# Two context attentions of a perceiver block: a later settle and a lag of two, weighted values by halves, denominators copied out of PSUM, pools that wait by tile

## The chip, the cores and the metric

The kernel runs on one core of a Trainium2 chip. A core has a matrix engine (TensorE, in the profile PE for the multiplications and PEld for the loads of the stationary operand), a vector engine (VectorE, DVE), a scalar engine (ScalarE, ACT), a general engine (GpSimd, POOL) and a queue for transfers (SyncE, SP). Each engine works through its own instructions in order; an instruction waits on semaphores for what it needs. Matrix products land in PSUM, a small memory of eight banks; everything else on the core lies in SBUF.

The metric is the device time of one execution in microseconds. Before the change three runs took 1695.6, 1703.4 and 1700.06 us, with a median of 1700.06.

## The reference

Two layers work on 512 tokens of width 512 (`x`), with a context of 8192 tokens of the same width. Everything is float32. Each layer adds three things to `x`, each after a layer norm: an attention over the context, an attention among the tokens, and a mixture of eight experts of which each token uses two. Cut to the part that is changed:

```python
x = x + L0_xattn(layernorm(x), ctx, padding_mask)   # 16 heads of 32, queries and keys normed per head
x = x + L0_attn(layernorm(x))                       # each token sees itself and later ones
x = x + L0_ffn(layernorm(x))                        # top 2 of 8 experts, width 2048
x = x + L1_xattn(layernorm(x), ctx, mask)           # 16 heads of 32, no norm of the keys
x = x + L1_attn(layernorm(x))                       # a band of 64 neighbours
x = x + L1_ffn(layernorm(x))                        # top 2 of 8 experts, width 1024

def xattn(q, y):                                    # both context attentions
    s = einsum("bihd,bjhd->bhij", heads(q), heads(k(y))) * scale
    p = softmax(where(allowed, s, -inf))
    return einsum("bhij,bjhd->bihd", p, heads(v(y))) @ Wo.T + bo
```

The masks come as data. With the inputs of this case only a small part of the context can be seen by any token.

## The kernel before

**Slots.** The kernel finds out at run time which tiles of 128 context tokens hold anything that may be seen. It has room for 15 such tiles, the *slots* (`SLOTS`), and gathers them; `tile_list` (L568) builds the list of tiles from counts. The list for layer 1 needs all of that layer's mask, which `MaskScan` (L1185) reads piece by piece during layer 0's key loop (the squares on ACT that find out whether a column is the same for all queries); its `finish` (L1216) and `tile_list` make the list. If 15 slots are not enough, another path runs under a branch at the end (L2028); it is not taken here.

**The order of stages**, in the profiled execution: queries and constants up to about 78 us; layer 0's key loop to about 213; its attention to about 484; self-attention to about 640; experts to about 935; layer 1's context attention to about 1365, of which the key loop runs to about 1100; self-attention to about 1478, and experts to the end.

**attend_slots** (L742) is called by both context attentions (`cross_slots0`, `cross_slots1`) with functions of the caller. Heads come in `NG` = 4 groups of `GH` = 4; the four heads of a group are four small products that run beside each other in the array, and such a set is called a *quad* here. An f32 product of 512 columns is two records (two passes) in the profile, so a quad is eight records.

- *Key loop.* For every slot s: `keys(s)` projects the keys (in layer 0: a product in the bank "acc", and DVE adds the bias into `kb`, L1055), `settle` transposes the normed keys of an earlier slot (`ktp`, L1064) and ACT writes them to `kT`, `maxima(0, ...)` multiplies an earlier slot's keys with the queries of group 0 and DVE takes the running maximum of the scores (`take`, L768 and L770), `values` projects the values (`pv`, L1016), and `unit(s)` norms the keys (a square on ACT, then DVE; its last step is L1109). In layer 1 there is no norm, `keys` writes `kT` itself, and `settle` and `unit` do nothing. `beside()` is the mask scan in layer 0.
- *After the loop* the last settles, maxima and values follow, and the first parts of `shift_of(0)` (L646): eight transposes of the maxima for each of its two parts (`mtp`), reductions on DVE (`neg`), a split of the maximum into three bf16 parts on POOL, and a last transposition (`stp`) that yields `shift`, three rows to be subtracted from the scores by a small product.
- *60 attention steps* (L891), one for each group g and slot i. The first 41 are *combined*: two halves j, in each of which PE makes a quad of two score heads of group g (`sc`) and two score heads of a later group (`scm`, for its maxima), then two small products that subtract the shift (L644); ACT takes the exponentials of the two heads into `pT` (L874), DVE the two maxima. The `sc` tiles have four PSUM banks, the `scm` tiles three, `acc` one. In the last 19, *plain* steps, PE makes the four score heads of g alone.
- `accumulate` (L821) multiplies the exponentials of the step before with the values: a quad over all 512 queries into `acc`. After a group's last slot ACT copies `acc` to `o` (L836).
- `add_up` (L838) adds the exponentials of four slots into one tile (POOL, in the last group DVE), so that `denominators` (L850) has to sum only four tiles per group by products with ones (`den`, in one of the four banks of `sc`).
- *Fillers* run at the end of a step, one at most: the parts of the next group's shift, the denominators (three steps after the end of a group), two reciprocals by halves (`divide`, L861), the output projections (`ops`, L717), and in layer 0's steps from 2 on a piece of layer 1's list (`listing`, L1084). In the last group a part of the denominators is made at the end of the last two steps.

**Pools.** Tiles come from pools that open and close with the stages. When a pool is opened where a closed one lay, its tiles wait for the users of what lay there before.

Of the kernel before, what the change touches and what calls it, by code (L numbers as in the profile page):

```python
# [57 lines left out]
def tile_perceiver(  # L58
# [6 lines left out]

    const = ctx.enter_context(tc.tile_pool(name="const", bufs=1))
# [9 lines left out]
    dram = ctx.enter_context(tc.tile_pool(name="dram", bufs=1, space=bass.MemoryType.DRAM))  # L76
# [22 lines left out]
    with tc.tile_pool(name="begins", bufs=1) as tmp, tc.tile_pool(name="beginsps", bufs=1, space=PSUM) as tps:  # L99
# [322 lines left out]
    def cross_attention0():  # L422
        with ExitStack() as st:
            pool = st.enter_context(tc.tile_pool(name="c0", bufs=2))
            ctxp = st.enter_context(tc.tile_pool(name="ctxp0", bufs=2))
            psum = st.enter_context(tc.tile_pool(name="c0ps", bufs=2, space=PSUM))
            pacc = st.enter_context(tc.tile_pool(name="c0acc", bufs=1, space=PSUM))
# [3 lines left out]
            with tc.tile_pool(name="c0q", bufs=2) as qp:  # L431
# [8 lines left out]
            kvp = st.enter_context(tc.tile_pool(name="c0kv", bufs=NCHUNK // 2))  # L440
# [70 lines left out]
    def cross_attention1():  # L511
        with ExitStack() as st:
            pool = st.enter_context(tc.tile_pool(name="c1", bufs=2))
            ctxp = st.enter_context(tc.tile_pool(name="ctxp1", bufs=2))
            psum = st.enter_context(tc.tile_pool(name="c1ps", bufs=2, space=PSUM))
            pacc = st.enter_context(tc.tile_pool(name="c1acc", bufs=1, space=PSUM))
# [3 lines left out]
            with tc.tile_pool(name="c1q", bufs=2) as qp:  # L520
# [7 lines left out]
            kvp = st.enter_context(tc.tile_pool(name="c1kv", bufs=NCHUNK))  # L528
            mp = st.enter_context(tc.tile_pool(name="c1m", bufs=2))
# [38 lines left out]
    def tile_list(tmp, psum, counts, bad, tag, out):  # L568
# [8 lines left out]
        nc.tensor.transpose(tp, counts, ident)  # L577
        nc.vector.tensor_copy(rows, tp)
# [4 lines left out]
        nc.tensor.matmul(ps, lhsT=tri, rhs=some, start=True, stop=True)  # L583
        place = tmp.tile([n, 1], F32, name="place", tag="place")
# [7 lines left out]
        nc.tensor.matmul(ps[:, SLOTS : SLOTS + 1], lhsT=ones[0:n, 0:1], rhs=some, start=True, stop=True)  # L592
        row = tmp.tile([1, SLOTS + 1], F32, name="row", tag="row")
# [10 lines left out]
        ps = psum.tile([P, SLOTS], F32, name="kbp", tag=tag)  # L604
        nc.tensor.matmul(ps, lhsT=rows, rhs=taken, start=True, stop=True)
        kbias = small.tile([P, SLOTS], F32, name="kbias", tag="kbias")
        nc.vector.tensor_scalar(kbias, ps, 1.0, BIG, ALU.subtract, ALU.mult)
# [134 lines left out]
    def attend_slots(pool, psum, pacc, kT, vN, qT, kbias, wo, bv, late, keys, settle, values, unit, more, early, aside, beside, extra):  # L742
# [47 lines left out]
        for s in range(n):  # L790
            keep(keys, s)
            if s >= 1:
                settle(s - 1)
            if s >= 2:
                maxima(0, s - 2)
            if (s + 1) * loop // n > s * loop // n:
                keep(values, todo.pop(0))
            unit(s)
            if s == 3:
                aside()  # L800
            beside()
        settle(n - 1)
        steps = shift_of(0)
# [3 lines left out]
        keep(values, todo.pop(0))  # L807
# [11 lines left out]
        last = None  # L819

        def accumulate():  # L821

            if last is None:
                return
            g, i, pT = last
            if i == 0:
                k.sums[g] = pacc.tile([P, S], F32, name="acc", tag="acc")
            for h in range(GH):
                nc.tensor.matmul(  # L829
                    k.sums[g][HD * h : HD * (h + 1), :],  # L830
                    lhsT=vN[:, i, g * P + HD * h : g * P + HD * (h + 1)],
                    rhs=pT[:, h, :], start=(i == 0), stop=(i == n - 1),
                )
            if i == n - 1 and g < NG - 1:
# [15 lines left out]
        def denominators(g, which, end):  # L850

            for j in which:
                if j == 0:
                    dens[g] = psum.tile([P, S], F32, name="den", tag="s")
                for h in range(GH):
# [3 lines left out]
                    )  # L859

        def divide(g, i):  # L861

            r = slice(i * S // 2, (i + 1) * S // 2)
            if i == 0:
                dens[g, 0] = late().tile([P, S], F32, name="d", tag="d", bufs=1)
# [1290 lines left out]
```

## Time and profile before

| | |
|---|---|
| median of three runs | 1700.06 us |
| the profiled execution's own time | 1700.19 us |
| its span | 1698.5 us |
| mean granted clock of TensorE | 0.938 |
| layer 0 key loop, 78 to 213 us: PE busy, PEclk, DMA share | 122.24 of 135.00, 0.94, 0.43 |
| layer 0 attention, 213 to 406: PE busy, PEclk | 190.14 of 193.00, 0.97 |
| its end, 406 to 484: PE busy, PEclk | 71.03 of 78.00, 0.96 |
| between experts and layer 1's keys, 935 to 965: PE busy, PEclk | 20.10 of 30.00, 0.83 |
| layer 1 attention, 1100 to 1284: PE busy, PEclk | 183.17 of 184.00, 0.98 |
| its end, 1284 to 1365: PE busy, PEclk | 73.79 of 81.00, 0.94 |

Busy time of an engine is the time in which at least one of its instructions ran; PE counts as busy while products run, and PEclk is the share of its full clock that was granted. In a stage where PE is busy for nearly the whole time, the pace may still be set by a wait within a quad, since one late head of four leaves the other three running. A line of the waits view names the waiting instruction, what it waited for, the sum, the number of times and the longest. In the timeline view a line is a run of like instructions: start, length, engine, line, operation, output and inputs, shapes and their number, and in brackets the idle time before and what ended it. In the windows view each engine's busy time in a stretch stands in the order PE, PEld, DVE, ACT, POOL, each with its number of instructions in brackets, then PEclk, the DMA engines' mean share and GB/s.

### The profile page before, as it was taken

How to read it: one execution, taken by the hardware profiler on the slowest of the kernel's cores; microseconds unless marked ns; L12 is line 12 of the kernel's file. 1: busy time of each engine (PE TensorE's matmuls, PEld its weight loads, DVE VectorE, ACT ScalarE, POOL GpSimd, SP SyncE). 2: the span in 40 equal slices, each digit the busy share in tenths (PEclk: the TensorE clock that was granted, in tenths of full speed). 3: DMA queues.
4: the chain of work that ended last, by engine and by line, in shares of the span. 5: the costliest groups of instructions: out<-in, count | busy, mean ns of one | idle time of the engine just before them, and what ended most of it. 6: DMA issues, size and time to landing. Idle time of an engine off the chain costs nothing. (4 is left out here: it accounts for less than half of the span.)

```text
span 1698.5 us, 24206 instructions
## 1 busy us (share of the span) xinstructions
PE 1559.3 (92%) x9877; PEld 908.3 (53%) x9877; DVE 775.3 (46%) x1394; ACT 570.7 (34%) x1081; POOL 446.5 (26%) x345
## 2 busy tenths in 40 slices
PE   5888999999979996999999799999999989779996
PEld 2333333333234446999998456433333245369995
DVE  5466677774633655111112133667765526831112
ACT  1356355556622231111111211155556612211110
POOL 6000057787110011000002100078786010010002
PEclk9999989999989977999999899899999989879996
DMA  7145200000030004877784400000000040066572
GB/s 249 50 136 180 74 1 1 1 1 1 1 131 1 1 1 177 326 257 267 284 293 155 156 26 19 25 1 1 1 1 1 1 152 11 25 237 216 187 246 92
DMA packets 83928, 169.32 MB, mean 100 GB/s; under 512 B 5106, under 2 KB 20498, under 8 KB 82384
## 3 DMA queue, kind: packets, MB, share of 16 engines
q1 hardware_dynamic: 77200, 147.87, 25.4%
q0 software_dynamic: 6016, 17.55, 3.0%
q10 hardware_dynamic: 576, 2.10, 0.4%
q8 instruction: 84, 1.38, 0.3%
q14 instruction: 52, 0.43, 0.1%
HBM read 156.82 MB, written 9.63 MB: 98 GB/s over the span
## 5 line engine op out<-in xcount | busy, mean ns | idle before, releaser
L874 ACT ACTIVATE pT<-sc,kbias 128x512 f32<-128x512 f32 x480 | 299.4, 687 | 205.3 <-PE sc L644 142.8
L757 PE MATMUL sc<-qTf,kTf 32*128 32x512 f32 x1264 | 299.4, 660 | 6.1 <-DVE d L866 4.9
L770 DVE SCALAR_TENSOR_TENSOR mx<-scm,kbias,mx 128x512 f32<-128x512 f32 x312 | 215.4, 743 | 98.2 <-PE scm L757 95.8
L757 PE MATMUL scm<-qTf,kTf 32*128 32x512 f32 x656 | 241.2, 654 | 2.1 <-DVE mx L770 2.1
L1801 PE MATMUL y<-hT,w 128*128 128x112 f32 (+13 forms) x1536 | 211.0, 297 | 0.6 <-DVE hT L1976 0.6
L1785 PE MATMUL hps<-tokens,w 128*128 128x112 f32 (+13 forms) x1536 | 208.5, 295 | 0.0
L1801 PEld LDWEIGHTS y<-hT,w 128*128 128x128 f32 x1536 | 204.3, 197 | 2.5 <-DVE hT L1976 0.8
L1785 PEld LDWEIGHTS hps<-tokens,w 128*128 128x128 f32 x1536 | 201.5, 195 | 1.7
L847 POOL TENSOR_TENSOR four<-four,pT 128x2048 f32<-128x2048 f32 x42 | 190.7, 4540 | 9.7 <-ACT pT L874 6.7
L757 PEld LDWEIGHTS sc<-qTf,kTf 32*128 32x128 f32 x1264 | 91.3, 190 | 147.8 <-issue 111.5
L847 POOL TENSOR_TENSOR four<-pT 128x2048 f32<-128x2048 f32 x24 | 109.0, 4544 | 109.2 <-ACT pT L874 109.2
L829 PE MATMUL acc<-pT,vNf 128*32 128x512 f32 x960 | 133.7, 623 | 1.5 <-ACT o L836 1.5
L770 DVE SCALAR_TENSOR_TENSOR mx<-sc,kbias,mx 128x512 f32<-128x512 f32 x136 | 93.3, 744 | 80.3 <-PE sc L757 80.3
L1976 DVE TENSOR_TENSOR hT<-sg,hps 128x264 f32<-128x264 f32 (+7 forms) x64 | 28.0, 437 | 189.5 <-ACT sg L1975 189.5
L644 PE MATMUL sc<-shift,ones 3*128 3x512 bf16 (+3 forms) x544 | 100.1, 383 | 3.6 <-DVE shift L679 3.6
L757 PEld LDWEIGHTS scm<-qTf,kTf 32*128 32x128 f32 x656 | 75.0, 188 | 49.8 <-DVE mx L770 38.0
L1826 POOL DMA_DIRECT2D answers_d<-yb x17 | 9.5, 559 | 311.5 <-ACT yb L1819 311.4
L1975 ACT ACTIVATE sg<-hps 128x264 f32<-128x264 f32 (+7 forms) x64 | 25.4, 397 | 137.4 <-PE hps L1785 137.4
L829 PEld LDWEIGHTS acc<-pT,vNf 128*32 128x32 f32 x960 | 20.7, 109 | 88.0 <-issue 80.6
L658 DVE TENSOR_REDUCE neg<-mtp 128x4 f32<-128x512 f32 x64 | 41.2, 683 | 53.8 <-PE mtp L655 53.8
L1981 DVE TENSOR_TENSOR hT<-sg 128x224 f32<-128x224 f32 (+7 forms) x32 | 14.7, 459 | 107.6 <-ACT sg L1980 107.6
L1016 PE MATMUL pv<-wkvf,cslot 128*128 128x512 f32 x120 | 59.1, 639 | 0.2 <-ACT vNf L1025 0.2
(340 smaller groups left out, 1833.8 us busy)
## 6 DMA issues: line engine op xcount, KB each, us to landing
w<-in_L_ffn_W SPq DMA_DIRECT2D x96, 1024.0 KB, 7.4
mi<-in_mask SPq DMA_DIRECT2D x32, 512.0 KB, 4.2
cslot<-in_ctxT SPq DMA_DIRECT2D x30, 256.0 KB, 4.9
answers_d<-yb POOLq DMA_DIRECT2D x15, 256.0 KB, 7.1
answers_d<-zero POOLq DMA_DIRECT2D x9, 256.0 KB, 6.6
wkvf<-in_L_xattn_WkvT ACTq DMA_DIRECT2D x4, 512.0 KB, 6.5
wq<-in_L_xattn_WqT SPq DMA_DIRECT2D x2, 1024.0 KB, 7.5
wof<-in_L_xattn_WoT SPq DMA_DIRECT2D x2, 1024.0 KB, 4.7
```

Source lines behind the costliest of these rows:

```text
L644: nc.tensor.matmul(ps, lhsT=ones16[r, :], rhs=k.shifts[g][r, 0:w], start=start, stop=stop)
L658: nc.vector.tensor_reduce(neg[:, h, :], tp.rearrange("p (t k) -> p t k", k=P), AX.X, ALU.max, negate=True)
L757: nc.tensor.matmul(ps, lhsT=kT[HD * h : HD * (h + 1), g, i * P : (i + 1) * P], rhs=qT[HD * h : HD * (h + 1), g, :], start=True, stop=stop,)
L770: nc.vector.scalar_tensor_tensor(to, ps, b, to, ALU.add, ALU.max)
L829: nc.tensor.matmul(k.sums[g][HD * h : HD * (h + 1), :], lhsT=vN[:, i, g * P + HD * h : g * P + HD * (h + 1)], rhs=pT[:, h, :], start=(i == ...
L847: engine.tensor_tensor(to, parts[g][-1], pT, ALU.add)
L874: nc.scalar.activation(pT[:, h, :], ps, AF.Exp, bias=kbias[:, i : i + 1])
L1016: last = nc.tensor.matmul(ps.rearrange("p (g n) -> p g n", g=NG), lhsT=src[:, c, s % 2, :], rhs=wkv[:, :, c, i * P : (i + 1) * P], start=( ...
L1785: nc.tensor.matmul(ps[:, j, 0:k], lhsT=w1[:, c, f * P : (f + 1) * P], rhs=tokens[:, c, starts[r] : starts[r] + k], start=(c == 0), stop=(c ...
L1801: nc.tensor.matmul(accs[0][:, d, 0:k], lhsT=w2[:, f, d * P : (d + 1) * P], rhs=hT[:, f, 0:k], start=(c == 0 and f == 0 and d % 2 == 0), st ...
L1975: nc.scalar.activation(sg, ps, AF.Sigmoid)
L1976: nc.vector.tensor_tensor(dst, sg, ps, ALU.mult)
```

## The change

The change touches both context attentions and the kind of wait between pools.

1. Nearly all pools are opened with `reuse_waits="tile"`: a new tile then waits only for those users of earlier tiles that touched its own bytes (in PSUM, its own bank), and no longer for all users of the pool that was there.
2. In the key loop the settle comes two slots after the keys instead of one, and the maxima three slots after instead of two. `kb` has three buffers instead of two. What follows the loop is reordered; the first part of `shift_of(0)` stands directly behind the last maxima.
3. In combined steps `accumulate` covers half of the queries behind each of the two quads, where one product over all queries stood behind the first. In plain steps it works on the exponentials of two steps before, and `pT` has five buffers instead of four. The last group's last denominators come ahead of the last `accumulate`.
4. For the first three groups ACT copies the finished denominators from PSUM to an SBUF tile `d`, and the reciprocals work in place on it.
5. The list of layer 1's tiles is cut into more fillers: a product of PE and the DVE instruction that reads it are in different steps, and one product (`kbp`) is made earlier. The fillers go from six to nine.

```diff
+    def tile_pool(**kw):
+        return tc.tile_pool(reuse_waits="tile", **kw)
...
         nc.tensor.transpose(tp, counts, ident)
+        yield
         nc.vector.tensor_copy(rows, tp)
...
         nc.tensor.matmul(ps, lhsT=tri, rhs=some, start=True, stop=True)
+        yield
         place = tmp.tile([n, 1], F32, name="place", tag="place")
...
         nc.tensor.matmul(ps[:, SLOTS : SLOTS + 1], lhsT=ones[0:n, 0:1], rhs=some, start=True, stop=True)
+        keep = psum.tile([P, SLOTS], F32, name="kbp", tag=tag)
+        nc.tensor.matmul(keep, lhsT=rows, rhs=taken, start=True, stop=True)
+        yield
         row = tmp.tile([1, SLOTS + 1], F32, name="row", tag="row")
...
-        ps = psum.tile([P, SLOTS], F32, name="kbp", tag=tag)
-        nc.tensor.matmul(ps, lhsT=rows, rhs=taken, start=True, stop=True)
...
         for s in range(n):
             keep(keys, s)
-            if s >= 1:
-                settle(s - 1)
             if s >= 2:
-                maxima(0, s - 2)
+                settle(s - 2)
+            if s >= 3:
+                maxima(0, s - 3)
...
+        settle(n - 2)
+        steps = shift_of(0)
+        maxima(0, n - 3)
+        keep(values, todo.pop(0))
         settle(n - 1)
-        steps = shift_of(0)
         maxima(0, n - 2)
         keep(values, todo.pop(0))
         maxima(0, n - 1)
-        keep(values, todo.pop(0))
         steps[0]()
         keep(values, todo.pop(0))
         steps[1]()
...
-        def accumulate():
-            if last is None:
+        def accumulate(lag, halves=(0, 1)):
+            if len(behind) < lag:
                 return
-            g, i, pT = last
-            if i == 0:
+            g, i, pT = behind[0]
+            r = slice(halves[0] * S // 2, (halves[-1] + 1) * S // 2)
+            if i == 0 and halves[0] == 0:
                 k.sums[g] = pacc.tile([P, S], F32, name="acc", tag="acc")
             for h in range(GH):
                 nc.tensor.matmul(
-                    k.sums[g][HD * h : HD * (h + 1), :],
+                    k.sums[g][HD * h : HD * (h + 1), r],
                     lhsT=vN[:, i, g * P + HD * h : g * P + HD * (h + 1)],
-                    rhs=pT[:, h, :], start=(i == 0), stop=(i == n - 1),
+                    rhs=pT[:, h, r], start=(i == 0 and halves[0] == 0), stop=(i == n - 1 and halves[-1] == 1),
                 )
+            if halves[-1] == 0:
+                return
+            behind.pop(0)
...
+            if g < NG - 1:
+                d = late().tile([P, S], F32, name="d", tag="d", bufs=1)
+                nc.scalar.copy(d, dens[g])
+                dens[g] = d
...
-            if i == 0:
-                dens[g, 0] = late().tile([P, S], F32, name="d", tag="d", bufs=1)
-            nc.vector.reciprocal(dens[g, 0][:, r], dens[g][:, r])
+            nc.vector.reciprocal(dens[g][:, r], dens[g][:, r])
...
-            pT = late().tile([P, GH, S], F32, name="pT", tag="pT", bufs=4)
+            pT = late().tile([P, GH, S], F32, name="pT", tag="pT", bufs=5)
...
-                    if j == 0:
-                        accumulate()
+                    accumulate(1, (j,))
...
-                accumulate()
+                accumulate(2)
...
-        accumulate()
+        accumulate(1)
         denominators(NG - 1, range(end - 2, end), end)
+        accumulate(1)
...
-                kb = kvp.tile([P, D], F32, name="kb", tag="kb")
+                kb = kvp.tile([P, D], F32, name="kb", tag="kb", bufs=3)
...
-                more, EARLY, aside, scanned, [listing] * 6,
+                more, EARLY, aside, scanned, [listing] * 9,
```

Inside the scan's `finish` one more `yield` stands between a transposition (`lbp`) and the DVE reduction that reads it. `late()` opens, at its first call after the key loop, the pool in which `pT`, `o`, `d` and the sums of four live, where the key loop's pools lay, and starts the load of the output weights.

## The prediction

> **What bounds the kernel now.** Busy time comes first, then the granted clock along the span (40 slices of 42.5 us).
>
> ```profile
> PE 1559.3 (92%) x9877; PEld 908.3 (53%) x9877; DVE 775.3 (46%) x1394; ACT 570.7 (34%) x1081; POOL 446.5 (26%) x345
> PEclk9999989999989977999999899899999989879996
> ```
>
> TensorE is the bound almost everywhere, so a change pays where PE stands still, or runs at half clock after standing still. The chain of waits covers the end of the program alone. I therefore read PE's waits stage by stage. First the layer 0 key loop (78 to 213 us), then the end of its attention (406 to 484).
>
> ```profile
> PE ktp L1064 <- DVE kb L1109: 12.0, 7, 3.1
> ```
>
> ```profile
> PE ops L717 <- DVE o L691: 4.3, 2, 2.9
> PE sc L757 <- DVE d L866: 1.8, 1, 1.8
> PE acc L829 <- ACT o L836: 0.7, 1, 0.7
> ```
>
> Columns: total us, times, longest. A short wait drags a slower clock behind it; the windows table, whose column PEclk reads 0.50, shows four such windows (length, then busy PE):
>
> ```profile
> 88.10:94.90 6.80, 6.35 (x16) 2.74 (x17) 4.19 (x7) 3.71 (x9) 0.91 (x3) 0.50 0.86 289
> 139.30:142.70 3.40, 3.40 (x11) 1.11 (x4) 2.07 (x4) 3.31 (x8) 0.43 (x2) 0.50 0.78 231
> 436.30:443.10 6.80, 6.80 (x30) 1.59 (x34) 1.95 (x1) 2.42 (x4) 4.64 (x2) 0.50 0.00 0
> 1316.90:1320.30 3.40, 3.40 (x17) 0.81 (x20) 0.69 (x1) 2.25 (x4) 3.30 (x2) 0.50 0.00 0
> ```
>
> Last, the timeline of PE and of DVE in an ordinary combined step:
>
> ```profile
> 334.12 1.06 PE L829 MATMUL acc<-pT,vNf 128*32 128x512 f32 x8
> 335.11 0.70 PE L757 MATMUL sc<-qTf,kTf 32*128 32x512 f32 x2
> 336.09 0.59 PE L757 MATMUL sc<-qTf,kTf 32*128 32x512 f32 x2
> 336.73 1.10 PE L757 MATMUL scm<-qTf,kTf 32*128 32x512 f32 x2
> 338.19 1.06 PE L829 MATMUL acc<-pT,vNf 128*32 128x512 f32 x8
> ```
>
> ```profile
> 336.33 1.41 DVE L770 SCALAR_TENSOR_TENSOR mx<-scm,kbias,mx 128x512 f32<-128x512 f32 x2 [1.34 <-PE scm L757]
> ```
>
> Acc to acc is 4.07 us. Two score quads stand back to back (335.11, 336.09). The fourth "scm" of the pair needs a bank that DVE's take from 336.33 gives up, and starts only at 337.14, or 2.02 after the first quad's start.
>
> **The change, part by part.**
>
> *Settle one slot later.* A settle transposes the keys that DVE has just normalised (L1109); with one more slot between, the result is there a whole slot (some 8 us) earlier than needed, and the 12.0 us go. So do the two half-clock windows of this loop, worth half their length at most: 3.4 + 1.7. Most is 17. What could be late next: per slot PE has about 7.8 us of work, ACT 70.7/15 = 4.7, DVE 86.0/15 = 5.7, with the mask transfers at 43% of the DMA engines; none reaches PE. I take 15, with 12 and 17 as ends. Layer 1's settle is empty: nothing.
>
> *Loop end.* steps[0] now stands right behind the last maxima; its transposes wait for DVE's takes (the first 1.16 us after the scores, 0.74 each), which a value projection of 3.6 us covered. Lost about 1.3 in each attention (1.1 to 1.6): -2.6.
>
> *Halves.* Self-attention's quad over 256 queries is the nearest row: its two passes stand 0.24 and 0.31 us apart, 0.55 in all, against 0.996 for 512. Two halves cost 0.10 more than a whole. A combined step's own work is then 2 x (0.96 scores + 0.31 subtracts + 0.55) = 3.64. Quads follow each other by 1.82, so the wanted bank comes 2.02 - 1.82 = 0.20 after the quad begins; the late score's own 1.05 to its end then sets 1.25, against the 1.27 of the undisturbed path. Hidden: 3.64; not hidden, each quad is late by half of the 0.20, as the next then starts later too: 3.84. DVE's four takes (2.97) and ACT's four exponentials (2.75) fit beneath. I take 3.75. There are 25 plain-looking 4.07 steps in layer 1 and 20 in layer 0, and five with the listing: 50 x 0.32 = 16. Steps with other work had hidden it in the 0.6 of stall and lose cover: four with outputs (5.44 to 5.61), two with denominators (7.08 to 7.24), two with reciprocals, two with the copy of o, in each attention; I put the loss at 3.1 an attention. Net 16 - 6 = **10** (4 to 15).
>
> *Denominators copied by ACT.* Six copies of 0.60 us (the price of ACT's 512-wide copies). They give the "s" bank back before the two reciprocals of 1.75 each, the 1.8 us wait above. In combined steps ACT is half idle, and the copy only delays the reciprocals (in the 3.1 above). In plain steps ACT is the bound (4 x 0.60 = 2.41 a step, PE 2.28), so the copy costs its 0.60.
>
> *Lag of two in plain steps, the last acc behind the last denominators.* Layer 0's steps 47 to 49 take 5.74 + 5.86 + 4.77 = 16.4. Denominators 3.6 + PE's 2.28, two steps at 2.41, and two ACT copies make 11.9: 4.5 less, of which 3.4 is half clock. Layer 1: 14.85 to 11.9. The four steps about the outputs (13.97) become PE's own 4 x 2.28 + 3.95 = 13.1, or 0.7 after a margin; two transposing steps 3.70 to 3.30, 0.8; at the end a reciprocal runs beside the last acc, 1.0. Sum 7.0 and 5.5: **12.5** (8 to 14). The wait of acc for the copy of o stays.
>
> *Listing by more fillers.* Layer 0's steps 3 to 7 take 7.4 us more than five at 4.07. The timeline says why:
>
> ```profile
> 240.91 4.58 DVE L588 TENSOR_SCALAR taken<-steps,place,some 64x15 f32<-64x15 f32 x1
> 249.78 3.55 DVE L601 TENSOR_TENSOR row<-row,none 1x1 f32<-1x1 f32 x1
> ```
>
> ```profile
> 240.94 4.53 POOL L847 TENSOR_TENSOR four<-pT 128x2048 f32<-128x2048 f32 x1 [3.15 <-ACT pT L874]
> 248.81 4.52 POOL L847 TENSOR_TENSOR four<-four,pT 128x2048 f32<-128x2048 f32 x1 [3.33 <-ACT pT L874]
> ```
>
> Two tiny DVE instructions stand until POOL's add ends, with the takes behind them and PE behind these. Here the Trainium skill speaks against the change: "SBUF — State Buffer", section "Who interferes with whom", says that DVE and GpSimd share a port pair under an exclusive lock, taken by two-port copies and scalar operations and by DVE instructions with two SBUF inputs. By it more yields remove neither wait; they only move PE's waits for DVE. By the row alone (7.4 over the even pace) I would book 7. With the new places, "taken" falls in a step without an add, some 2 us before the running one ends, and "row" meets one by chance. I book **5** (2 to 6.5).
>
> The same page lets a DVE instruction with one SBUF input, outside such modes, run free. That matters for the reciprocals, which now read SBUF beside POOL's adds. The trace shows no such reciprocal there; nearest is the reduce of "crow" from SBUF, 278 ns beside an add and 278 without. I take nothing; the upper end is a whole add, 4.5 us, for each of 12, and below nothing there is no reason.
>
> *Pools by tile.* Weights for self-attention may start some 11 us earlier, but after both attentions PE waits for the layer norm's DVE chain, not weights: 0 to 1, taken 0. After the first ffn, Wq of layer 1 is issued at 934.37 and lands at 940.32; DVE branches at 935.52 and goes on at 940.34, in spite of no semaphore on Wq. If DVE's code waits behind that megabyte, an issue some 6 us earlier shortens this; ACT's same branch took 2.47 before the transfer, PE's branch at the end of the program 3.9 without one. Gain 0 to 4.7, taken **2**. Expert weights wait for routing: nothing.
>
> **Sum.** 15 - 2.6 + 10 + 12.5 + 5 + 2 = 41.9. From the profiled execution's own 1700.2 (span 1698.5; the median of the three runs is 1700.06, practically the same): 1658. I forecast **1659**.
>
> The clock is where I chose the trace over the skill. "TensorE: Matmul & The Clock Gate", section "Why this matters for your kernels", warns of idle gaps above about 3 us. By that only the 3.1 us wait costs clock, and the sum gets 3.4 of clock in all, 1666. But half-clock windows here follow waits of 2.4, 1.79 and 1.81 us as well; by the rows all go, 10.2 in all.
>
> **Rivals.** (a) *The halves return nothing.* The bank wait survives in another form, or longer DVE work after the copies does; combined steps only pay their lost cover. 10 becomes -6: 1700.2 - 25.9 = 1674. For it: takes fill four fifths of DVE's step (2.97 of 3.75). Against: equal spacing is exactly what the bank wants. Chance 0.20. (b) *The loop finds a new bound.* Squares on ACT mix with the mask scan, with 134 GB/s of transfers; the loop gains 5, not 15: 1668. For it: PE's longest waits coincide with DMA shares of 0.78 to 0.86; against: the averages above. Chance 0.14. (c) *Reciprocals out of SBUF are shut out by POOL's adds.* Place: the step behind each group's denominators, with takes behind the reciprocals. In the listing 8.13 us of such blocking cost about 6.8 of excess, 0.84 per us; twelve full adds cost 12 x 4.53 x 0.84 = 46, giving 1704, slower than before by little. It decides from 41.9/(12 x 0.84) = 4.2 us per reciprocal, nearly always a whole add; the "crow" row is against it. Chance 0.04. (d) *The change doesn't reach the waits*: lag and pools leave the loop as it is, and gains shrink to the plain steps, 1688. PE's order of instructions in the changed program does have the settle behind another slot's keys; 0.04.
>
> **Numbers.** The forecast has 0.58. Its parts at their good ends add to 17 - 2.2 + 15 + 14 + 6.5 + 5.7 = 56, at their poor ends to 12 - 3.2 + 4 + 8 + 2 + 0 = 23: 1644 to 1677, with (a) and (b) inside. The range stops at 1643 and 1680. About 0.5%, 8.5 us, is what a measurement here tells from no change: faster means below 1691.6, which (d) mostly keeps. Faster 0.94, same 0.03, slower 0.03.
>
> **What would show it.** Right: no PE wait on L1109 in the loop, which lasts about 120 us; combined steps of 3.64 to 3.84; the wait on the denominators' bank and the half clock behind it gone from the plain steps; reciprocals still 1.75; DVE's "taken" still long when an add runs. Wrong: combined steps at 4 or above, a new wait of PE on ACT or on takes in the loop, reciprocals of several us, or new half-clock windows behind the moved transposes at the loop's end.

## The result and the profile after

The changed kernel takes 1690.91 us (median of 18 runs, 1685.35 to 1702.68), the kernel before 1701.07 (18 runs). The ratio is 0.9948, with a 95% interval of 0.9932 to 0.9964: 10 us were gained, where 41 had been forecast, and the time lies outside the range of 1643 to 1680. The profiled execution took 1687.45 us (span 1685.6). First the page's busy times and granted clock:

```profile
PE 1541.9 (91%) x10517; PEld 920.6 (55%) x10517; DVE 780.9 (46%) x1394; ACT 572.2 (34%) x1087; POOL 450.1 (27%) x345
PEclk9999899999989896999999899989999999779996
```

PE is busy for 17 us less, and its share hardly moved: waits went, others came, and the clock is no better than before. That last point decides how the numbers are read. The records give the stretches in which half the clock was granted. A stage's length less half of that time is my estimate of what it would have taken at full clock, and is meant where the text says "at full clock". It supposes that PE sets the pace throughout such a stretch. In layer 0's experts, where half-clock time ran from 16.6 to 42.3 us over all profiles of this case, it gives 283.9 to 290.5, with the largest figures where the half clock was shortest; so there it can be some 5 us off. The table gives lengths in us, with the half-clock time of each in brackets, for the kernel before, the changed kernel, and a second profile of the same changed kernel; the last two columns are the first two at full clock.

| stage | before | after | after, again | before, full clock | after, full clock |
|---|---|---|---|---|---|
| start, to the first key projection | 42.57 (0) | 42.38 (0) | 42.20 (0) | 42.6 | 42.4 |
| keys, to the first exponential | 173.19 (25.3) | 165.13 (12.8) | 165.38 (16.7) | 160.6 | 158.7 |
| layer 0, combined steps | 192.85 (8.9) | 187.83 (14.5) | 196.08 (31.0) | 188.4 | 180.6 |
| layer 0, plain steps | 64.69 (6.8) | 62.81 (3.4) | 61.11 (0) | 61.3 | 61.1 |
| layer 0, its end | 14.00 (0) | 14.96 (3.4) | 15.45 (3.4) | 14.0 | 13.3 |
| self-attention | 156.59 (30.7) | 158.23 (30.7) | 160.36 (37.5) | 141.2 | 142.9 |
| experts and join | 300.35 (30.1) | 305.22 (42.1) | 303.84 (33.4) | 285.3 | 284.2 |
| layer 1, keys | 157.17 (13.8) | 160.57 (17.2) | 158.51 (11.7) | 150.3 | 152.0 |
| layer 1, combined steps | 186.54 (7.3) | 178.92 (8.9) | 182.18 (16.3) | 182.9 | 174.5 |
| layer 1, plain steps | 63.15 (3.4) | 62.77 (3.4) | 62.74 (3.4) | 61.5 | 61.1 |
| layer 1, its end | 16.20 (6.8) | 14.90 (3.4) | 15.95 (6.8) | 12.8 | 13.2 |
| self-attention, experts, end | 331.18 (77.8) | 331.89 (81.2) | 331.80 (78.0) | 292.3 | 291.3 |
| span | 1698.5 (210.9) | 1685.6 (221.2) | 1695.6 (238.4) | 1593.0 | 1575.0 |

At full clock the change takes off 18.0 us, nearly all of it in the combined steps (7.8 + 8.4) and the keys of layer 0 (1.9). Half-clock time rose by 10 us in one profile and by 28 in the other, which by the same estimate gave back 5 and 14.

**Where the gain came as forecast.** The timeline of PE in an ordinary combined step of the changed kernel:

```profile
320.33 0.70 PE L764 MATMUL sc<-qTf,kTf 32*128 32x512 f32 x2
321.61 0.64 PE L839 MATMUL acc<-pT,vNf 128*32 128x256 f32 x8
322.18 0.70 PE L764 MATMUL sc<-qTf,kTf 32*128 32x512 f32 x2
323.45 0.64 PE L839 MATMUL acc<-pT,vNf 128*32 128x256 f32 x8
324.02 0.70 PE L764 MATMUL sc<-qTf,kTf 32*128 32x512 f32 x2
```

From quad to quad 1.84 to 1.85, and 3.69 us from step to step, against 4.07: evenly spaced, and all but hidden. A half product takes 0.57 (321.61 to 322.18).

**Where it went.** PE's waits in the key loop (69 to 208 us):

```profile
PE pv L1031 <- ACT vNf L1040: 5.0, 2, 2.6
PE pk L1031 <- DVE kb L1070: 4.6, 4, 1.4
PE mtp L662 <- DVE mx L777: 0.9, 1, 0.9
```

The 12.0 us of waits for the normed keys are gone, but 9.6 of others stand in their place. ACT's waits in the same stretch point to the cause. The first line is of the changed kernel, the second of the kernel before (70 to 216 us), where the wait was there already:

```profile
ACT un_v L181 <- DVE un_v L180: 27.9, 12, 2.8
```

```profile
ACT un_v L177 <- DVE un_v L176: 33.2, 14, 3.2
```

The timelines of ACT and DVE in the changed kernel show one turn of it, with some lines of ACT left out:

```profile
161.75 0.62 ACT L1120 ACTIVATE un_q<-kb 128x512 f32<-128x512 f32 x1
165.18 0.22 ACT L181 ACTIVATE un_v<-un_v 128x16 f32<-128x16 f32 x1 [2.81 <-DVE un_v L180]
165.30 0.71 ACT L1225 ACTIVATE square<-mi,first 128x512 f32<-128x512 int32 x1
...
167.74 0.56 ACT L1040 COPY vNf<-pv 128x512 f32<-128x512 f32 x1
```

```profile
162.40 0.69 DVE L1122 TENSOR_REDUCE un_s<-un_q 128x16 f32<-128x512 f32 x1 [2.24 <-ACT un_q L1120]
163.00 2.06 DVE L777 SCALAR_TENSOR_TENSOR mx<-sc,kbias,mx 128x512 f32<-128x512 f32 x3
164.98 0.17 DVE L180 TENSOR_SCALAR un_v<-un_s 128x16 f32<-128x16 f32 x1
```

ACT squares the keys, and has nothing to do until DVE has reduced them and also run three takes that stand before `un_v` in its queue. Only then come ACT's root, three of its four squares of the mask scan and the copy of the values that PE waits for. In this turn each engine stands idle for over 2 us, for the other. Neither is busy for two thirds of the loop: of its 138.45 us DVE works 90.07 and ACT 77.68.

In layer 0's plain steps (waits from 395 to 473 us):

```profile
PE ops L724 <- POOL o L886: 3.2, 1, 3.2
PE ops L724 <- DVE o L698: 3.1, 2, 2.1
```

The wait for the denominators' bank is gone, and the output products wait for POOL's `o` instead. The timeline of POOL and DVE there:

```profile
423.11 2.23 DVE L860 TENSOR_TENSOR four<-four,pT 128x2048 f32<-128x2048 f32 x1
423.34 3.13 POOL L884 TENSOR_TENSOR o<-o,d 128x512 f32<-128x512 f32 x1 [7.97 <-DVE d L881]
426.43 2.29 DVE L860 TENSOR_TENSOR four<-pT 128x2048 f32<-128x2048 f32 x1 [1.09 <-ACT pT L889]
426.56 3.59 POOL L886 TENSOR_SCALAR o<-o,bvC 128x512 f32<-128x512 f32 x1
```

POOL's two instructions take 1.27 and 1.58 us in combined steps. Here each begins 0.1 to 0.2 us after an add of DVE has begun, and ends 1.1 and 1.4 us after that add has ended. Step 51 took 9.0 us, and the four steps about the outputs (50 to 53) 18.5.

In the listing the wait moved too (DVE, then POOL):

```profile
248.12 4.36 DVE L608 TENSOR_TENSOR none<-none,bad 1x1 f32<-1x1 f32 x1
```

```profile
247.95 4.51 POOL L860 TENSOR_TENSOR four<-pT 128x2048 f32<-128x2048 f32 x1 [2.34 <-ACT pT L889]
```

Another instruction with two SBUF inputs meets an add. Steps 3 to 10 exceed the new pace by 9.0 us, where steps 3 to 7 had exceeded the old one by 7.4; with 6.8 and 3.4 us of half clock in them, that is 5.6 and 5.7 at full clock. Finally, PE's wait at the join behind layer 0's experts, in the kernel before and in the changed one:

```profile
PE lnt L197 <- DVE xn L194: 9.9, 1, 9.9
```

```profile
PE lnt L201 <- DVE xn L198: 7.6, 1, 7.6
```

### The profile page after: what moved, and what is told of

Read it like the earlier page. It is cut to its first block, busy times and chain, and to the rows that moved or that the text cites. A ratio compares the mean times of both kernels' runs of the same rounds, so it can differ in the third digit from the quotient of the medians.

```text
span 1685.6 us, 25397 instructions
## 1 busy us (share of the span) xinstructions
PE 1541.9 (91%) x10517; PEld 920.6 (55%) x10517; DVE 780.9 (46%) x1394; ACT 572.2 (34%) x1087; POOL 450.1 (27%) x345
## 5 line engine op out<-in xcount | busy, mean ns | idle before, releaser
L777 DVE SCALAR_TENSOR_TENSOR mx<-scm,kbias,mx 128x512 f32<-128x512 f32 x312 | 219.3, 745 | 72.3 <-PE scm L764 69.8
L764 PE MATMUL scm<-qTf,kTf 32*128 32x512 f32 x656 | 224.0, 669 | 10.2 <-DVE mx L777 10.2
L764 PEld LDWEIGHTS sc<-qTf,kTf 32*128 32x128 f32 x1264 | 83.7, 187 | 121.3 <-issue 78.1
L839 PE MATMUL acc<-pT,vNf 128*32 128x256 f32 (+1 forms) x1600 | 146.6, 438 | 1.6 <-ACT o L849 1.6
L839 PEld LDWEIGHTS acc<-pT,vNf 128*32 128x32 f32 x1600 | 32.1, 108 | 133.6 <-issue 127.8
L651 PE MATMUL sc<-shift,ones 3*128 3x512 bf16 (+3 forms) x544 | 94.7, 380 | 3.6 <-DVE shift L686 3.6
```

The costliest lines, as they stand in the source:

```text
L651: nc.tensor.matmul(ps, lhsT=ones16[r, :], rhs=k.shifts[g][r, 0:w], start=start, stop=stop)
L764: nc.tensor.matmul(ps, lhsT=kT[HD * h : HD * (h + 1), g, i * P : (i + 1) * P], rhs=qT[HD * h : HD * (h + 1), g, :], start=True, stop=stop,)
L777: nc.vector.scalar_tensor_tensor(to, ps, b, to, ALU.add, ALU.max)
L839: nc.tensor.matmul(k.sums[g][HD * h : HD * (h + 1), r], lhsT=vN[:, i, g * P + HD * h : g * P + HD * (h + 1)], rhs=pT[:, h, r], start=(i == ...
```

## The experiments

Each is an edit of the changed kernel. Where no number of runs is given there was one, and the reading is of stages in its profile.

**The key loop as before** (`lag_one`):

```diff
-            if s >= 2:
-                settle(s - 2)
-            if s >= 3:
-                maxima(0, s - 3)
+            if s >= 1:
+                settle(s - 1)
+            if s >= 2:
+                maxima(0, s - 2)
```

with the loop's end and the two `kb` buffers as before. "The stretch" is the one from the first key projection of layer 0 to its first exponential.

> The changed kernel with the key loop, its end and the two kb buffers as before. Theory A, a ring of ACT and DVE had set the pace of this loop before as well, and the lag of two took away only what PE lost beyond it: the stretch from the first key projection to the first exponential goes back from 165.1 us to 171 to 175, with PE waiting some 12 us for the normed keys, and everything behind it keeps its length but for windows of half clock. Theory B, the lag gained nothing and something else shortened the loop: it stays at 163 to 167.

The stretch took 169.4 us, short of the 171 foreseen, with PE waiting for the normed keys again:

```profile
PE ktp L1077 <- DVE kb L1122: 12.3, 7, 3.1
```

At full clock it is 160.7, against 154.7 to 158.7 in the nine profiles that keep the lag of two and this order of the squares. So the lag is worth 2 to 6 us at full clock.

**The squares in the gap** (`squares_between`): the mask scan runs inside `unit_rows`.

```diff
         nc.scalar.activation(sq, src, AF.Square)
+        if between:
+            between()
```

> The changed kernel with the mask scan's squares of a slot issued between the two ACT steps of the key norm (square, then root) instead of behind them. Theory A, a ring of ACT and DVE sets the key loop: ACT now stands 2.8 us per slot at the root, which waits for DVE's reduction and three takes, and only then runs its four squares (3.7 us). With the squares in that gap a slot loses up to 2.8 us of the ring's 7.6 to 8, PE becomes the bound of the loop, and the stretch from the first key projection to the first exponential goes from 165.1 us (of it 12.8 at half clock) to 152 to 158; PE's waits on the value copy (5.0) and on the key bias (4.6) go. Theory B, the one bank of the key projection sets the loop: those waits stay and the stretch keeps within 2 us.

The stretch fell to 157.7 us, just inside the range, and to 151.5 at full clock. ACT's wait in the loop became

```profile
ACT un_v L181 <- DVE un_v L180: 3.8, 2, 2.8
```

and PE's waits on values and keys fell from 9.6 to 3.9. The ring of ACT and DVE had set the pace. Moving work into its gap gives 3 to 7 us at full clock against the same nine profiles, 5.4 against their mean of 156.9; the later kernels with this order give 149.2 to 151.2.

**Outputs two steps later, and o on DVE** (`outputs_later`, `o_on_dve`):

```diff
-                    (at + 7, lambda g=g: k.outputs(g, (0, 1))),
-                    (at + 8, lambda g=g: k.outputs(g, (2, 3))),
+                    (at + 7 + 2 * (g == NG - 2), lambda g=g: k.outputs(g, (0, 1))),
+                    (at + 8 + 2 * (g == NG - 2), lambda g=g: k.outputs(g, (2, 3))),
```

```diff
-            nc.gpsimd.tensor_tensor(k.o[g], k.o[g], dens[g], ALU.mult)
-            nc.gpsimd.tensor_scalar(k.o[g], k.o[g], bv[:, g : g + 1], None, ALU.add)
+            engine = nc.vector if g == NG - 2 else nc.gpsimd
+            engine.tensor_tensor(k.o[g], k.o[g], dens[g], ALU.mult)
+            engine.tensor_scalar(k.o[g], k.o[g], bv[:, g : g + 1], None, ALU.add)
```

> The changed kernel with the last two output fillers (those of group 2, in the plain steps) two steps later. Theory A, these products now come before GpSimd has finished o (PE stood 3.2 us, then ran at half clock): the wait goes, step 51 falls from 9.0 to 2.3 and the plain steps from 62.8 us to 56.5 to 59 in both attentions. Theory B, the output projections cost what they cost wherever they stand and the wait comes from elsewhere: 61 or more.

> The changed kernel with the multiplication and the bias of group 2's o on DVE instead of GpSimd, in program order with DVE's own adds. Theory A, GpSimd's two instructions on o stand behind DVE's adds at the shared port (3.13 and 3.59 us, against 1.27 and 1.58 in combined steps): on DVE they take some 0.7 and 0.5 us, the products at step 51 wait at most 1 us, and the plain steps fall from 62.8 to 57 to 59.5. Theory B, the chain of denominators, copy and reciprocals alone is too late for the products at that step: PE still waits 2 us or more for o, and the plain steps stay above 60.5.

Both came as theory A says: the plain steps took 57.9 us in both attentions in both kernels, with no half clock in them, instead of 62.8. With `o` on DVE the four steps about the outputs take 13.6. On DVE, in the order of its own adds, the two instructions take

```profile
428.46 0.69 DVE L885 TENSOR_TENSOR o<-o,d 128x512 f32<-128x512 f32 x1
429.18 0.49 DVE L886 TENSOR_SCALAR o<-o,bvC 128x512 f32<-128x512 f32 x1
```

and PE waits 0.6 us there, for another instruction of DVE. So the chain of copy and reciprocals is in time, and POOL's standing behind DVE's adds is what made it late: the exclusive lock that the section on interference in the Trainium skill's page "SBUF — State Buffer" ("Who interferes with whom") describes, here with DVE first and POOL blocked.

**The list's small instructions on POOL** (`list_on_pool`):

```diff
-        nc.vector.tensor_scalar(taken, steps[0:n, 0:SLOTS], place, some, ALU.is_equal, ALU.mult)
+        engine = nc.vector if bad is None else nc.gpsimd
+        engine.tensor_scalar(taken, steps[0:n, 0:SLOTS], place, some, ALU.is_equal, ALU.mult)
+        yield
```

and so for `none`, the added row and `irow`; the comparison of the two counts moves to the end of the program.

> The changed kernel with the list's small SBUF instructions (taken, none, the added row, the integer row) on GpSimd, where they queue behind the adds, one more filler step for the product that reads taken, and the comparison of the two counts made at the end. Theory A, DVE stands behind GpSimd's adds at the shared port: attention steps 3 to 10 of layer 0, 38.6 us in sum now (10.26 of it in step 10), fall to 29.5 to 31.5, and the combined steps of layer 0 from 187.8 to 179 to 182. Theory B, the products of the list cost PE its time: the sum stays above 36.

Steps 3 to 10 took 31.2 us, as foreseen; PE's wait of 3.0 us is gone. The stage as a whole (187.1) did not reach 179 to 182. Half clock is a part of that (17.0 us). The other part is that the longer list put the next group's maximum one step off, and its split came late behind an add on POOL:

```profile
PE stp L684 <- POOL mparts L675: 2.2, 1, 2.2
```

Steps 14 and 15 took 6.8 and 4.8 instead of 4.0 and 3.7, with 3.4 us of half clock in them.

**Whole products again** (`whole_acc`):

```diff
-                    accumulate(1, (j,))
+                    if j == 0:
+                        accumulate(1)
```

> The changed kernel with the weighted values of a combined step in one product over all queries behind the first half, as before. Theory A, halves space the quads as DVE's takes need it: undone, an ordinary combined step goes from 3.69 back to 4.07 us, and layer 1's combined steps from 178.9 to 184 to 188 us. Theory B, the gain there came from the lag of the reading or from the five pT buffers: steps stay at 3.7 to 3.8.

Ordinary steps are back at 4.07 us. Layer 1's combined steps took 192.2, more than foreseen, with 19.1 us of half clock; at full clock 182.7, the 182.9 of before. The halves are the whole of the 8.4 us gained there. This kernel took 1703.2, no less than before.

Its plain steps, whose code is that of the changed kernel, came out shorter: 58.7 us in both attentions, without half clock. PE waited 0.8 us for POOL's `o` instead of 3.2:

```profile
435.55 1.56 POOL L886 TENSOR_SCALAR o<-o,bvC 128x512 f32<-128x512 f32 x1
```

```profile
435.77 2.61 DVE L860 TENSOR_TENSOR four<-pT 128x2048 f32<-128x2048 f32 x1 [1.44 <-ACT pT L889]
```

Here POOL's second instruction began 0.22 us ahead of DVE's add and took its usual time; in the changed kernel it began 0.13 us behind the add (426.56 against 426.43) and took 3.59. So most of the loss in the plain steps hung on which of the two came first by a fraction of a microsecond.

**Without ACT's copies** (`no_d_copy`):

```diff
-            if g < NG - 1:
-                d = late().tile([P, S], F32, name="d", tag="d", bufs=1)
-                nc.scalar.copy(d, dens[g])
-                dens[g] = d
```

with the reciprocals reading the bank.

> The changed kernel with the reciprocals reading the denominators in their bank, without ACT's copy. Theory A, the copy only pays in the plain steps: there PE waits again some 1.8 us for the bank and the three steps from 47 on go from 10.7 back to 13 or more (a step may fall to half clock), while the two combined steps with reciprocals fall from 6.4 to 5.5 to 5.8 each; an attention's sum changes by less than 2 us. Theory B, the copy also helps combined steps: these rise as well, and each attention is over 3 us longer.

In layer 0's plain steps the bank wait came back (2.1 us), the wait for POOL's `o` went, behind slower steps, and the plain steps took 60.9 at full clock, as with the copy: in the changed kernel the copy had only changed one wait for another. Layer 1's combined steps fell from 174.5 to 173.0. Of the four steps with reciprocals only one was within the 5.5 to 5.8 foreseen; the others took 7.4 to 8.3, with half clock in them. The copies for groups 0 and 1 lose time because they stand ahead of the reciprocals. The first line is DVE's in the changed kernel, the second the same place without the copy:

```profile
290.61 3.37 DVE L881 RECIPROCAL d<-d 128x256 f32<-128x256 f32 x2 [3.40 <-ACT d L875]
```

```profile
290.63 3.37 DVE L879 RECIPROCAL d<-den 128x256 f32<-128x256 f32 x2 [2.79 <-PE den L869]
```

In both the two reciprocals stand back to back. They begin 4.30 us after the first product of the denominators with the copy (286.31) and 3.68 without it (286.95): 0.62 later, the length of the copy. The step is 0.6 us longer, too (6.36 and 5.75, the one such step without half clock). POOL and PE of the changed kernel at that place:

```profile
288.25 4.53 POOL L860 TENSOR_TENSOR four<-four,pT 128x2048 f32<-128x2048 f32 x1
```

```profile
294.60 0.69 PE L764 MATMUL scm<-qTf,kTf 32*128 32x512 f32 x1 [1.76 <-DVE mx L777]
```

The takes stand behind the reciprocals and PE behind the takes. The first reciprocal ran beside POOL's add in its usual 1.75, as all reciprocals out of SBUF did in every profile (1.69 to 1.75). Rival (c) is out, and the rule of the Trainium skill ("SBUF — State Buffer", section "Who interferes with whom") that a DVE instruction with one SBUF input, outside the two-port modes, runs free of GpSimd holds for the reciprocals of this trace.

**Pools as before** (`pools_as_before`):

```diff
-        return tc.tile_pool(reuse_waits="tile", **kw)
+        return tc.tile_pool(**kw)
```

> The changed kernel with pools that wait for all users of closed pools. Theory A, it earns only in the join behind the first mixture of experts, where Wq of layer 1 is issued earlier and PE's wait went from 9.9 to 7.6 us: the wait goes back to 9.5 to 10.2 and the stretch from there to layer 1's first exponential is 2 to 3 us longer; other stages keep their length at full clock within 1 us. Theory B, it earns at the starts of self-attention or of the attention steps too: those stages are 2 us or more longer at full clock.

The wait at the join is 10.1 us again. The stretch from there to layer 1's first exponential was not 2 to 3 us longer (152.5 and 152.0 at full clock), and the experts with the join took 285.3, inside the spread of the other profiles (283.9 to 290.5). Self-attention and experts of layer 1 are 2 and 1 us longer, but stages differ by as much between the two profiles of the unaltered kernel. So the wait of 2.5 us is shown, and any gain of the pools beyond it stays open.

**The same kernel again** (`after_again`).

> The changed kernel once more, unaltered. If half-clock windows fall [...]not by the code alone, stages come out with other lengths than in the first profile (layer 0's experts 298 to 306 us, layer 0's combined steps 187 to 196), while each stage's length less half its half-clock time agrees within 1 us. If they belong to the code, the stages repeat.

The half clock did not repeat. Most stages came within 1 us at full clock; layer 0's keys (157.0 and 158.7), its self-attention (141.6 and 142.9), its experts (287.2 and 284.2) and layer 1's self-attention (105.4 and 103.6) did not. One place in both profiles, the wait of 1.8 us behind the reciprocals of group 0, in the windows view (the column before the last two is PEclk; the first line is the first profile, the second the second):

```profile
292.80:303.60 10.80, 9.04 (x88) 3.26 (x86) 8.58 (x12) 5.52 (x9) 7.39 (x3) 1.00 0.00 0
```

```profile
294.80:305.60 10.80, 9.04 (x55) 2.80 (x58) 6.36 (x9) 3.56 (x6) 7.36 (x3) 0.68 0.00 0
```

The same wait, and a stretch of half clock behind it in one execution and none in the other. Over the ten profiles that show this wait (1.76 to 1.83 us, four in each), half clock set in within 2.4 us of its end in 23 of 40 cases, and in 13 of 14 cases about the waits of 3.15 us or more for POOL's `o`.

**The copy for group 2 alone** (`copy_once`), with the other reciprocals reading their bank, to see whether these four waits explain the half clock:

```diff
-            if g < NG - 1:
+            if g == NG - 2:
```

> The changed kernel, but ACT copies only the denominators of group 2 (plain steps); the reciprocals of groups 0 and 1 read their bank as before. Theory A, the copies of groups 0 and 1 cost 1.5 us an attention at full clock and, by the half clock behind their four waits, some 6 us more on average: median 1680 to 1686 against the changed kernel's 1690.9. Theory B, half clock saved there turns up elsewhere: 1686 to 1690, the 3 us at full clock alone or less.

The median was 1687.4 (six runs), ratio to before 0.9907 (0.9886 to 0.9929). By the medians that is 3.5 us below the changed kernel, as theory B says; by the ratios, each to runs of the kernel before from its own session, it is some 7, as theory A says. So the runs leave it open. The profile says more: at the four places PE's recorded wait is shorter (0.69 to 0.76 us), and half clock stands behind all four. The first of them:

```profile
291.53 0.66 PE L764 MATMUL sc<-qTf,kTf 32*128 32x512 f32 x1 [0.69 <-DVE d L883]
```

In the four profiles without these copies, 13 of 16 such places had half clock behind them, no fewer than with the waits of 1.8 us. What the copies cost is therefore their 3 us at full clock; a saving of half clock is not shown.

**The mends together** (`three_mended`: the squares in the gap, the small instructions of the list on POOL, `o` of group 2 on DVE; then with the copy for group 2 alone `four_mended`; each measured a second time). So that the list puts nothing off, its fillers begin a step earlier:

```diff
-        fillers = list(enumerate(extra, 2))
+        fillers = list(enumerate(extra, 1))
```

> The changed kernel with the squares between the two ACT steps of the key norm, the list's small instructions on GpSimd (fillers from step 1 on, so that the next group's maximum isn't put off), and group 2's o on DVE. If the three causes found are separate, their gains add at full clock: key loop -5.5, list -3 to -6, plain steps -3.2 in each attention, and the half clock behind two of these waits goes: against the changed kernel's median of 1690.9 some 1672, range 1664 to 1680. If PE's stalls only move on, it stays above 1684.

> As three_mended, and ACT copies the denominators of group 2 alone (the plain steps), not those of groups 0 and 1. Undoing all copies made combined steps 1.5 us per attention shorter at full clock and brought PE's wait for the bank back in the plain steps; with the copy kept there both should be had: 3 us below three_mended, 1661 to 1677. If the copies of groups 0 and 1 don't matter, the two agree within 1 us at full clock.

> four_mended once more: under theory A below three_again by 5 to 10 us in the median, under theory B within 4 us of it.

> three_mended once more, on the same chip as four_again; median 1659 to 1669.

| | median us | ratio to before, 95% interval | profile at full clock |
|---|---|---|---|
| three_mended | 1664.0 (6 runs) | 0.9789 (0.9749 to 0.9830) | 1562.6 |
| four_mended | 1667.6 (6 runs) | 0.9793 (0.9758 to 0.9829) | 1559.3 |
| four_again | 1661.9 (5 runs) | 0.9767 (0.9746 to 0.9788) | 1555.9 |
| three_again | 1663.0 (5 runs) | 0.9773 (0.9751 to 0.9795) | 1559.3 |

Both are faster than either kernel, by some 2.2% against before. `three_mended` came out at the good end of its range: keys 149.2 to 151.2, layer 0's combined steps 176.2 to 176.4, plain steps 57.9, all at full clock. Between the two, the profiles show 3.3 and 3.4 us at full clock, some 2 of them in the combined steps. The medians do not: `four_mended` is 3.6 us above in the first pair and 1.1 below in the second, as theory B of `four_again` says.

## Why the prediction was wrong, step by step

Of the 41.9 us in the forecast's sum, 10.2 came. The table sets the terms against the stages, without clock (the mean of the two profiles of the changed kernel at full clock) and with the clock as a term of its own (what the medians lack of that gain):

| term | forecast, us | measured, us |
|---|---|---|
| layer 0's keys: settle, loop end | 8.6 | 2.7 |
| layer 1's keys: loop end | -1.3 | -2.0 |
| combined steps: halves, listing | 15 | 16.5 |
| plain steps and ends | 7.4 | 1.0 |
| experts and join | 2 | -0.4 |
| other stages | 0 | -0.5 |
| clock | 10.2 | -7.1 |

So the clock is the largest miss (17 us); the plain steps and the keys lack some 6 each, and within the combined steps the listing's loss is hidden by the halves.

*Settle one slot later, 15 us: failed.* The waits went, as said, and the stretch gained 8.1 in the profile with the loop's end in it, but 1.9 at full clock. The sentence that failed is "What could be late next: ... none reaches PE". It compared averages (4.7 and 5.7 us a slot against PE's 7.8) where the pace was set by a round of dependences through two queues, each waiting for the other. ACT's 33.2 us of waiting in the trace before would have shown it. Rival (b) had the right place and nearly the right loss, and the wrong cause: not transfers or the sum of ACT's work, but its order.

*Loop end, -2.6: right in kind.* The transposes waited 0.92 us in each attention, less than the 1.3 foreseen. The half clock that stands about the first attention steps (13.7 us in layer 0, 17.1 in layer 1) is no new one: it was there before with the same lengths.

*Halves, 10 us net: right, and too small.* The floor of 3.64 was nearly met (3.69), 0.05 above it; the lost cover was as foreseen in the steps with outputs and denominators (5.60, 7.12). The 8.4 us of layer 1's combined steps are the halves and the copies together; without copies it is 9.9, where 5 had been forecast for an attention. Rival (a) is out.

*The copies: priced at nothing in combined steps, beyond a share of the 3.1.* Each puts the reciprocals off by its own 0.6 us there; four of them cost some 3 us at full clock.

*Plain steps and end, 12.5 us: failed.* They gained 2.6, and 0.9 at full clock. Steps 47 to 49 did better than forecast (10.7 against 11.9): the two steps behind the denominators took PE's 2.3 and not ACT's 2.41, and ACT's copies were nearly hidden. The step that failed is "The four steps about the outputs (13.97) become PE's own 4 x 2.28 + 3.95 = 13.1": they took 18.5. The products came to a point where POOL, behind DVE's adds, had not finished. I had read the port rule into the listing and not asked where else DVE and POOL both work on SBUF: the last group's adds are on DVE, and POOL finishes group 2 beside them. The mends give 3.2 us at full clock, and 4.9 with the half clock, in each attention. `whole_acc` shows that a shift of some 0.3 us between the two engines would have spared most of it, so the size of the loss was in part bad luck.

*Listing, 5 us: failed.* The rule had been weighed rightly, and still the chance of a free moment was priced too high. With adds on POOL for 70% of these steps the next small instruction met one. At full clock layer 0's combined steps exceed layer 1's, which have no listing, by 5.5 us before and by 6.1 after: of the 5 nothing came. With the small instructions on POOL it is 4.4, and 2.1 in `three_mended`.

*Join, 2 us: right by the wait, not shown by the stage.* Wq was issued at 913.71 and had landed at 918.74, well before DVE's branch; DVE's idle time there fell from 5.5 to 3.2 us, and PE's wait by 2.4. So the load was a part of what DVE waited for, and the rest is open. The stage as a whole did not get shorter beyond its spread.

*The clock, 10.2 us in the sum: failed.* The rows did show half clock behind waits of 1.8 us, and more than half of the later waits of that length had it too; from the third attention step on, all half clock in the sixteen profiles begins near a wait of PE of 0.69 us or more. So for the place of half clock this trace was a better guide than the 3 us that the prediction cites. The step that failed is "by the rows all go, 10.2 in all": I booked windows of one execution as if they belonged to the waits that went. In the key loop and the plain steps half clock did fall (by the table from 25.3 to 12.8 and 16.7, and from 10.2 to 6.8 and 3.4), but it rose elsewhere: in the second profile by 31 us in the combined steps, in the first by 12 in the experts, which the change leaves alone. In all it is 221 and 238 us, against 211 before. By medians and full-clock sums it takes back about 7 us of the 17.3 gained (1593.0 to 1575.7, the mean of two profiles, against 10.2 in the medians). Why it falls where it does, and more of it after the change, is open.

The measured time is near the 1688 of rival (d), but by luck: the waits for the normed keys and for the denominators' bank did go, and (d) says that they stay.

## What to carry to other kernels

Before a wait is booked as gain, follow the chain that ended it once around through each engine's queue in order: two engines that are each half idle can still set the pace, and the cure is to put ready work into the gap, as the squares were. When steps get shorter, list what was timed to a step's number and ask whether its inputs keep up. Compare stages at full clock, and do not book half-clock windows of a single execution.

## What the runs showed that I had not expected

The same code, profiled twice, differed by 10 us in span, and by 1.4 at full clock (1685.6 and 1695.6; 1575.0 and 1576.4). In a stage that the change leaves alone, layer 0's experts, half clock ranged from 16.6 to 42.3 us over the profiles. And which of two engines began 0.1 to 0.2 us before the other decided over more than 2 us of an instruction of POOL.
